# Two-layer transformer on one core: expert gathers, row combinations, splines and norms of the second layer's attention, placed in smaller pieces over more steps

## The chip, the cores and the metric

The kernel runs on one core of a Trainium2 chip. The core has five engines with a queue each: TensorE (PE, with PEld for its weight loads), VectorE (DVE), ScalarE (ACT), GpSimd (POOL) and SyncE (SP, which issues most DMAs). An engine executes its queue in order, and instructions of different engines wait for each other through semaphores. The metric is the device time of one execution, in microseconds (us).

## The reference

The reference has two layers over `x` of 4 batches x 512 tokens x 256 features. Each layer modulates its norms with vectors computed from a small input, adds an attention part with a gate, and adds a feed-forward part with a gate.

- Layer 0: a linear attention part, then a mixture of experts. Every token goes to 6 of 32 experts, each expert takes at most 48 tokens, and the weighted rows of its six experts plus a shared expert are added up for each token. In short: `x = x + gb * y`, where `y` is the sum over six rows and the shared part.
- Layer 1: causal attention with 16 heads of 128, softmax and an output product, then a gated FFN. The three weight matrices of this FFN are not given; they are cubic splines through some 2000 control points, and have to be evaluated.

```
h = layernorm(x) * (1 + cb) + sb
x = x + gb * moe(h)                      # layer 0
h = layernorm(x) * (1 + ca) + sa
x = x + ga * attention(h)                # layer 1
h = layernorm(x) * (1 + cb) + sb
x = x + gb * (silu(h @ gate.T) * (h @ up.T)) @ down.T
```

All is computed in 32-bit floats. Tokens lie on partitions: a batch is 4 blocks (`NTT`) of 128 tokens, `xs[b]` is 128 x 4 x 256.

## The kernel before

Layer 0 runs first, up to about 250 us. Its last step is kept for later in parts: the weighted expert rows lie in `ytab` in HBM, and `code` holds which row belongs to which token and rank. For batch 0 the rows are added up in layer 0 already. For batches 1 to 3 that is done during the attention of layer 1, since a batch needs its `x` only when its own heads begin.

The attention of layer 1 is one loop over 64 heads, 16 for each batch, `for n in range(NHD + 1)` (L1504 and on). A pass of it is called a step here. A step of about 11.6 us computes the scores of head `n`, the projections of head `n + 1` (`project`, in four parts), the transposes and the weighted sum of head `n - 1`, a part of the values of the next four heads, and a part of the output product, `LAG` = 7 steps behind. Products of 256-wide blocks are done with seven block products in place of eight. The sums and differences of weight blocks that this needs are called forms; GpSimd makes them with `weight_forms` (L1161 to L1177): `w3` and `w2` of the next head after part 1 of a projection, `w1` and `w4` after part 3. TensorE reads `w3` and `w2` early in the next step (as `P1p` in the profile), and `w1`, `w4` later in it (as `P2p`). The forms have one buffer each, so the next ones wait until TensorE has read the last. `out_prepare` makes the forms for the output product (`oW`, `oF`, `oH`).

The order of TensorE is the order in the program (`manual_schedule`). On the other engines a planner orders the instructions by readiness and its own estimates; `tc.issue_after(x)` keeps an instruction from being placed ahead of `x` on its engine, without a wait. `evicted[n]` is the VectorE instruction that ends the projection of head `n`; it is executed at the end of step `n - 1`. `last_form[0]` is the last form `w1` that was made.

Besides the heads, a step carries pieces of other work:

- `gather(b, r, after)`, L278: the four row blocks of one rank `r` of batch `b`, by four indirect DMAs from GpSimd, each adding 128 rows of 1 KB into `ysum[b][:, i, :]`. Each waits for `evicted[n]`. Batch 1 has them at steps 1 to 6, batch 2 at 12, 13 and 18 to 21, batch 3 at 28, 29 and 34 to 37; so there are four gathers in a step, and the next gather into the same block comes with the next rank.
- `combine(b, after)`, L290: for each of the four blocks `ysum *= gate` and `x += ysum` on VectorE, at steps 10, 26 and 42.
- `norm(b)`, at steps 11, 27 and 43: the layer norm of the next batch (`ln_stats` takes means and variances of four blocks on VectorE, L192 and L193; the power -1/2 is taken on GpSimd, L196; then `xn`), its transposes, and `norm_forms`.
- `spline(u)`, L1118: one 128 x 256 tile of an FFN weight, on every second step from 6 to 52: a multiplication, three multiply-adds, two of half width, and transposes on TensorE at the end of the step. After units 1, 4 and 7 `ffn_forms` makes four forms on GpSimd.
- `ffn_norm(0)` at step 59 in the program. As nothing holds it, the planner places its statistics as soon as `x` of batch 0 is done, in steps 43 and 44.

The FFN of layer 1 follows, from about 1000 us to the end.

## Time and profile before

| what | value |
|---|---|
| median of three runs | 1174.84 us (1174.59 to 1176.95) |
| the profiled execution | 1174.33 us, of which the span 1172.6 us |
| TensorE busy, whole span | 1121.6 us, 96% |
| TensorE busy, 330 to 470 us | 139.27 of 140 us |
| TensorE busy, 470 to 520 us | 48.78 of 50 us |
| TensorE busy, 780 to 1000 us | 219.51 of 220 us |
| VectorE busy, 330 to 470 us | 116.48 of 140 us |
| GpSimd busy, 254 to 330 us | 60.02 of 76 us |
| granted TensorE clock | 0.988 over the span, 1.00 from 300 us on |

The span is the time from the first to the last instruction of the program in the profile. "Busy" is the time in which an engine executes; waiting and issuing are not in it. In lists of waits, "A <- B" means that A stood idle until B was done; when an instruction waits for several others, the last one by the profile is named. A matmul of 128 x 256 appears as two records, started 0.216 us apart; its shown length (0.38 us) overlaps the next one, so starts are what to compare. [...]

### The profile page before, as it was taken

To read this page: it belongs to the slowest core of one execution; us is meant where nothing else is said; L and a number is where in the kernel's file an instruction comes from. 1 tells how busy PE (TensorE), PEld (TensorE's weight loads), DVE (VectorE), ACT (ScalarE), POOL (GpSimd) and SP (SyncE) were. 2 spreads that over 40 slices of the span, in tenths; PEclk is the share of its full clock that TensorE was granted. 3 is DMA by queue.
4 is the path that set the end of the run, shared out by engine and by line. 5 is a ranking of instruction groups with operands and counts; after the bars stand their busy time and mean duration, and the time that the engine had idled before them with its cause. 6 is when DMAs were issued, how large, how long until landed. Compare 5 with 4: busy or idle time off the path is not lost.

```text
span 1172.6 us, 16886 instructions
## 1 busy us (share of the span) xinstructions
PE 1121.6 (96%) x5220; PEld 823.0 (70%) x5220; DVE 860.2 (73%) x2596; ACT 536.3 (46%) x1373; POOL 621.2 (53%) x945
## 2 busy tenths in 40 slices
PE   6888999879999999999999999999999999999998
PEld 2434354457777777777778777777777777888887
DVE  5688623467888788788887888888877677467765
ACT  3542223335555545554555555554555455333321
POOL 3354124328974856965565975444535655344331
PEclk9999899889999999999999999999999999999999
DMA  7801289734421312321221431011010000000001
GB/s 268 285 26 43 83 250 284 227 113 84 88 64 41 76 43 66 75 68 36 66 57 46 94 64 59 26 39 60 28 37 28 19 18 1 1 1 19 18 1 37
DMA packets 80486, 86.10 MB, mean 73 GB/s; under 512 B 12158, under 2 KB 64748, under 8 KB 80268
## 3 DMA queue, kind: packets, MB, share of 16 engines
q1 hardware_dynamic: 65564, 68.10, 18.6%
q0 software_dynamic: 11712, 13.25, 6.8%
q10 hardware_dynamic: 3120, 3.68, 1.0%
q8 instruction: 42, 0.69, 0.2%
q14 instruction: 48, 0.39, 0.1%
HBM read 73.84 MB, written 11.55 MB: 73 GB/s over the span
## 4 chain that ended last, share of the span: by engine, by line
PE 61%; DVE 9%; POOL 3%; ACT 3%; issue 1%; DMA 1%; SPq 0%; ACTq 0%; DVEq 0%; POOLq 0%
PE s L1293 10%; PE o L1334 9%; PE po L1029 7%; PE P0p L1029 6%; PE fP L1029 6%; PE pt L1325 5%; PE P1p L1029 4%; PE P2p L1029 3%; PE acc L1029 3%; PE P0v L1029 3%; PE P2v L1029 2%; PE P1v L1029 2%; POOL ysum L281 1%; DVE spw L1124 1%; DVE nm L1305 1%
## 5 line engine op out<-in xcount | busy, mean ns | idle before, releaser
L1308 ACT ACTIVATE p<-s,nm 128x512 f32<-128x512 f32 (+3 forms) x256 | 135.4, 529 | 117.1 <-DVE nm L1305 115.0
L1293 PE MATMUL s<-qk,qk 128*128 128x512 f32 (+3 forms) x512 | 170.2, 435 | 1.3 <-DVE qk L1201 1.0
L1334 PE MATMUL o<-pT,v 128*128 128x512 f32 (+3 forms) x512 | 148.6, 433 | 0.2 <-DVE u3v L1213 0.2
L1334 PEld LDWEIGHTS o<-pT,v 128*128 128x128 f32 x512 | 96.8, 190 | 55.0 <-issue 30.6
L1327 ACT COPY pT<-pt 128x512 f32<-128x512 f32 (+1 forms) x192 | 98.4, 513 | 68.2 <-PE pt L1325 66.4
L1305 DVE TENSOR_REDUCE nm<-s 128x1 f32<-128x512 f32 (+3 forms) x256 | 124.1, 485 | 4.0
L281 POOL DMA_INDIRECT ysum<-ytab,code x72 | 113.0, 1570 | 20.4 <-issue 15.5
L1310 DVE TENSOR_SCALAR p<-p,den 128x512 f32<-128x512 f32 (+3 forms) x256 | 117.6, 460 | 3.4
L1325 PEld LDWEIGHTS pt<-ident,p 128*128 128x128 f32 x640 | 81.7, 141 | 34.4 <-issue 10.5
L1325 PE MATMUL pt<-ident,p 128*128 128x128 f32 x640 | 101.7, 273 | 0.3 <-DVE p L1310 0.3
L1303 DVE TENSOR_TENSOR s<-s,mask 128x128 f32<-128x128 f32 x256 | 73.5, 287 | 31.2 <-PE s L1293 31.2
L1168 POOL TENSOR_TENSOR w_p<-w_q,w_k 128x128 f32<-128x128 f32 x63 | 38.7, 615 | 87.2 <-ACT t1p L1207 53.0
L1293 PEld LDWEIGHTS s<-qk,qk 128*128 128x128 f32 x512 | 77.5, 191 | 5.9 <-issue 1.5
L1029 PE MATMUL P0p<-hT_a,w_q 128*128 128x256 f32 x252 | 75.0, 379 | 0.0
L1176 POOL TENSOR_TENSOR w_p<-w_k 128x128 f32<-128x128 f32 x63 | 29.9, 475 | 81.0 <-PE P2p L1029 81.0
L1029 PEld LDWEIGHTS P0p<-hT_a,w_q 128*128 128x128 f32 x252 | 47.5, 190 | 33.1 <-issue 29.9
L1309 DVE RECIPROCAL den<-den 128x1 f32<-128x1 f32 x256 | 40.4, 158 | 38.4 <-ACT p L1308 33.6
L1029 PE MATMUL P1p<-fT,w_p 128*128 128x256 f32 x252 | 64.9, 380 | 2.4 <-POOL w_p L1170 1.2
L1345 ACT ACTIVATE oH<-o,bia 128x512 f32<-128x512 f32 x64 | 44.0, 687 | 42.1 <-PE o L1334 41.1
L1201 DVE SCALAR_TENSOR_TENSOR qk<-P0p,bia,u3p 128x256 f32<-128x256 f32 x63 | 30.4, 482 | 37.1 <-ACT qk L1222 36.1
L1037 POOL TENSOR_TENSOR fI<-it 128x256 f32<-128x256 f32 x30 | 21.8, 728 | 67.0 <-DVE it L1623 67.0
L1029 PEld LDWEIGHTS P1p<-fT,w_p 128*128 128x128 f32 x252 | 47.6, 190 | 9.9 <-issue 1.9
(338 smaller groups left out, 2683.2 us busy)
## 6 DMA issues: line engine op xcount, KB each, us to landing
wg<-in_w_gate_up SPq DMA_DIRECT2D x16, 704.0 KB
w_q<-in_w_q SPq DMA_DIRECT2D x64, 128.0 KB
w_k<-in_w_k SPq DMA_DIRECT2D x64, 128.0 KB
w_v<-in_w_v SPq DMA_DIRECT2D x16, 512.0 KB
wd<-in_w_down SPq DMA_DIRECT2D x16, 352.0 KB
basis<-in_basis SPq DMA_DIRECT2D x8, 640.0 KB
planes<-zero SPq DMA_DIRECT2D x4, 768.0 KB
yr<-planes SPq DMA_DIRECT2D x4, 768.0 KB
```

The lines of the kernel that those rows point to most:

```text
L281: ga = nc.gpsimd.indirect_dma_start(out=ysum[b][:, i, :], out_offset=None, in_=ytab[:, :], in_offset=bass.IndirectOffsetOnAxis(ap=code[:, ...
L1029: nc.tensor.matmul(out, lhsT=lhsT, rhs=rhs, start=start, stop=stop, skip_group_check=shared)
L1293: nc.tensor.matmul(s[:, at[i] : c], lhsT=qk[n, 0][:, i * P : (i + 1) * P], rhs=qk[n, 1][:, : (i + 1) * P], start=True, stop=True,)
L1303: nc.vector.tensor_tensor(s[:, e - P : e], s[:, e - P : e], mask, ALU.add)
L1305: nc.vector.tensor_reduce(nm, s[:, e - w : e], AX.X, ALU.max, negate=True)
L1308: nc.scalar.activation(p, s[:, e - w : e], AF.Exp, bias=nm, accum_out=den)
L1309: nc.vector.reciprocal(den, den)
L1310: nc.vector.tensor_scalar_mul(p, p, den)
L1325: nc.tensor.transpose(pt[:, c : c + P], probs[n, i][:, j * P : (j + 1) * P], ident)
L1327: nc.scalar.copy(pT, pt[:, :w])
L1334: nc.tensor.matmul(o[:, j * P :], lhsT=vs[n // 4][:, j, hc : hc + HD], rhs=pTs[n, j], start=(j == 0), stop=(j == NTT - 1),)
L1345: nc.scalar.activation(oT, o, AF.Identity, bias=bia[:, 2, h : h + 1])
```

## The change

Nothing is computed otherwise; where instructions stand is changed.

- `gather` handles one block and one rank, and no longer waits for `evicted[n]`. For each batch the 24 gathers are in the order block by block, the six ranks of a block after each other. At each step at most one is placed after part 2 of the projection, and up to three more after `out_prepare`. Batch 1 has 3, 3, 3, 3, 3, 3, 2, 2, 2 of them from step 0 on; batches 2 and 3 have 3, 3, 1, 1, 1, 1, 3, 3, 3, 3, 1, 1 from steps 12 and 28 on.
- `last_form[0]` is set after the early forms too, so what is placed after it may come behind `w2` as well.
- `combine` handles one block: at steps 3, 5, 7 and 10 for batch 1, at 15, 20, 22 and 25 for batch 2, at 31, 36, 38 and 41 for batch 3. It takes the block's statistics as well, and `ln_stats` uses them.
- `spline(u, part)`: the first three of its six operations are placed on the odd step before, the others and the transposes where the whole was.
- `ffn_forms` for the first three chunks: at steps 10, 26 and 42, after `last_form[0]`.
- `ffn_norm(0)` may not be placed ahead of `evicted[59]`.

```diff
     def ln_stats(b, name, after):
-        st = small.tile([P, NTT, 6], F32, tag="st", name=f"st_{name}{b}")
-        ag = small.tile([P, NTT, 2], F32, tag="ag", name=f"ag_{name}{b}")
-        with after_or_not(after):
-            for i in range(NTT):
-                nc.vector.bn_stats(st[:, i, :], xs[b][:, i, :])
-                nc.vector.bn_aggr(ag[:, i, :], st[:, i, :])
+        if b in stats:
+            _, ag = stats.pop(b)
+        else:
+            ...
-    def gather(b, r, after):
-
-        for i in range(NTT):
-            ga = nc.gpsimd.indirect_dma_start(
-                ...
-            )
-            wait_for(ga, [after])
-
-    def combine(b, after):
-
-        for i in range(NTT):
-            y, xi = ysum[b][:, i, :], xs[b][:, i, :]
-            with tc.issue_after(after.ins):
-                nc.vector.tensor_tensor(y, y, gbr[:, b, :], ALU.mult)
-                nc.vector.tensor_tensor(xi, xi, y, ALU.add)
+    def gather(b, i, r):
+
+        nc.gpsimd.indirect_dma_start(
+            out=ysum[b][:, i, :],
+            out_offset=None,
+            in_=ytab[:, :],
+            in_offset=bass.IndirectOffsetOnAxis(ap=code[:, b * NTT + i, r : r + 1], axis=0),
+            compute_op=ALU.add,
+        )
+
+    def combine(b, i, after):
+        ...
+        with tc.issue_after(after.ins):
+            nc.vector.tensor_tensor(y, y, gbr[:, b, :], ALU.mult)
+            nc.vector.tensor_tensor(xi, xi, y, ALU.add)
+            nc.vector.bn_stats(st[:, i, :], xi)
+            nc.vector.bn_aggr(ag[:, i, :], st[:, i, :])
@@
-        def spline(u):
+        def spline(u, part):
             r, j = divmod(u, 3)
             t, c = basis[r], win[:, j, r, :]
+            if part == 0:
+                w = spw[u] = sp.tile([P, D], F32, tag="spw", name=f"spw{u}")
+                nc.vector.tensor_scalar_mul(w, t[:, 1, :], c[:, 1:2])
+                for q in (2, 3):
+                    nc.vector.scalar_tensor_tensor(w, t[:, q, :], c[:, q : q + 1], w, ALU.mult, ALU.add)
+                return
+            w = spw.pop(u)
+            nc.vector.scalar_tensor_tensor(w, t[:, 4, :], c[:, 4:5], w, ALU.mult, ALU.add)
             ...
@@
-                nc.gpsimd.tensor_tensor(w2, A22, w3, ALU.subtract)
+                new_form = nc.gpsimd.tensor_tensor(w2, A22, w3, ALU.subtract)
                 wc[key] = {2: w2, 3: w3}
+                last_form[0] = new_form
@@
-        gathers = {r + 1: (1, r) for r in range(TOPK)}
-        for b in range(2, B):
-            for r, n in enumerate((-4, -3, 2, 3, 4, 5)):
-                gathers[(b - 1) * NH + n] = (b, r)
+        gathers, combined_at = {}, {}
+        for b in range(1, B):
+            todo, first_step = [(b, i, r) for i in range(NTT) for r in range(TOPK)], (0, 12, 28)[b - 1]
+            for n, m in enumerate((3, 3, 3, 3, 3, 3, 2, 2, 2) if b == 1 else (3, 3, 1, 1, 1, 1, 3, 3, 3, 3, 1, 1)):
+                gathers[first_step + n] = [todo.pop(0) for _ in range(m)]
+            for i, n in enumerate((3, 5, 7, 10) if b == 1 else (3, 8, 10, 13)):
+                combined_at[first_step + n] = b, i
+
+        def gather_some(n, m):
+            with tc.issue_after(last_form[0].ins):
+                for _ in range(min(m, len(gathers.get(n, ())))):
+                    gather(*gathers[n].pop(0))
@@
             project(n + 1, 2)
+            gather_some(n, 1)
@@
                 out_prepare(n)
+            gather_some(n, 3)
@@
+            if n % 2 and 5 <= n and unit < 3 * NCH:
+                with tc.issue_after(evicted[n].ins):
+                    spline(unit, 0)
+            if n in (10, 26, 42):
+                with tc.issue_after(last_form[0].ins):
+                    ffn_forms(n // 16, early[:, n // 16])
             if n % 2 == 0 and 6 <= n and unit < 3 * NCH:
                 with tc.issue_after(evicted[n].ins):
-                    spline(unit)
-                if unit in (1, 4, 7):
-                    ffn_forms(unit // 3, early[:, unit // 3])
+                    spline(unit, 1)
@@
-            if n in gathers:
-                gather(*gathers[n], evicted[n])
+            if n in combined_at:
+                combine(*combined_at[n], evicted[n])
             if n // NH + 1 < B:
-                if n % NH == 10:
-                    combine(n // NH + 1, evicted[n])
@@
-                ffn_norm(0)
+                ffn_norm(0, evicted[n])
```

## The prediction

> **What bounds the kernel now.** I read the page first, then TensorE's list of waits in the attention of layer 2, then busy time by stage, then the timeline at three places.
>
> The page (engine busy times, and the row of the gathers; columns of that row: line, engine, operation, out<-in, count | busy us, mean ns | idle before):
>
> ```profile
> span 1172.6 us, 16886 instructions
> ...
> PE 1121.6 (96%) x5220; PEld 823.0 (70%) x5220; DVE 860.2 (73%) x2596; ACT 536.3 (46%) x1373; POOL 621.2 (53%) x945
> ...
> L281 POOL DMA_INDIRECT ysum<-ytab,code x72 | 113.0, 1570 | 20.4 <-issue 15.5
> ```
>
> TensorE's waits from 300 to 1000 us (who <- for whom: us, times, longest):
>
> ```profile
> PE P2v L1029 <- DVE v L1200: 1.9, 1, 1.9
> PE P2p L1029 <- POOL oWTrue L1361: 1.2, 2, 0.7
> PE P1p L1029 <- POOL w_p L1170: 1.2, 1, 1.2
> PE P1p L1029 <- DVE x L248: 1.1, 2, 0.6
> PE s L1293 <- DVE qk L1201: 0.4, 2, 0.2
> PE pt L1325 <- DVE p L1310: 0.3, 1, 0.3
> ```
>
> TensorE is the bound: in 700 us it stands 6.1 us. So the change, which alters no matmul and no place in TensorE's or SyncE's order (the built programs agree there instruction by instruction), can win little. But every late VectorE or GpSimd result is paid in full.
>
> **The change part by part.** The profiled execution took 1174.33 us, of which 1172.6 are span. The three timed runs have the median 1174.84, 0.5 more. I sum on the span.
>
> *What is taken away.* The 1.2 us of `w_p L1170` come at 506.5: four steps in a row hold four gathers each (7.5 us of GpSimd at the pitch of 1.86 below), and four FFN forms (L1050 to L1053, about 2.4 us there) follow them, ahead of the forms that `P1p` needs. Afterwards the forms are at steps 10, 26 and 42, where no gathers stand: 1.2 won. The 1.9 us at 775.8 is a pile on VectorE: the FFN norm of batch 0, the norm of batch 3 and a spline, with a stand for GpSimd's power in it:
>
> ```profile
> 775.08 0.16 DVE L203 SCALAR_TENSOR_TENSOR nmr_f<-ag_f,rs_f 128x4 f32<-128x4 f32 x1 [0.91 <-POOL rs_f L196]
> ```
>
> The FFN norm moves to step 59, where no spline stands. I count 1.9 won and 0.4 lost again there. The two waits put down to `oWTrue` (385.7, 575.7) sit behind the same pile for batches 1 and 2 (GpSimd had ended; the VectorE read of that PSUM bank was late): statistics now come earlier but the trip to GpSimd for the power stays, so half, 0.6. The waits of `s` on `qk` come just after a spline of six operations in a row; halved splines win 0.3. `x L248` is the residual, untouched. Sum of waits 3.6; around the wait at 506 the matmul starts lose 1.39 for 1.22 of wait, so times 1.14: **4.1 us won** (bounds: 0, and 5.4 if all 4.7 go). VectorE's operations (multiply, add, statistics, splines) keep their number and size; only places move, so no busy time is added.
>
> *What is added: a chain of landings.* Before, a step issues the four row blocks of one rank. The next gather into the same block comes a step later. Now six gathers into one block follow each other, each adds into the same bytes, and in the built program each waits on the semaphore of the one before. What a gather takes until it has landed, the trace shows at the last gather of batch 3: GpSimd's timeline, then DMA share in 40 slices of 0.2 us from 692 to 700:
>
> ```profile
> 689.06 1.56 POOL L281 DMA_INDIRECT ysum<-ytab,code  x1 [0.30 <-issue]
> ...
> 692.79 1.56 POOL L281 DMA_INDIRECT ysum<-ytab,code  x1 [0.30 <-issue]
> 693.77 1.06 POOL L1168 TENSOR_TENSOR w_p<-w_q,w_k 128x128 f32<-128x128 f32 x1
> ...
> DMA  6676545665434333565544420000000000000000
> ```
>
> GpSimd is done after 1.6 us, but packets run to about 697.0, 4.2 us after the start, and the completion signals come after them. In the trace's records of these signals 44 of the 72 gathers have all sixteen: the last comes 4.29 to 6.06 us after the start, mean 4.85; for batch 1's own (266 to 327 us) the median is 4.6. I take landing 4.6 and a link from start to start of 4.75 (0.15 is the idle time that precedes a gather after other GpSimd work). The Trainium skill speaks against me here: "DMA: Bandwidth & Descriptors", section "Anatomy of one DMA — SWDGE (gpsimd) path", fits 2.0 us + bytes/436e3, for 128 KB an estimated 2.3 us. Counted from the start, a link would be shorter than the work between two gathers, the chain would cost nothing and the sum were -4.1. Counted from the end of the 1.56 us it would be 3.86, and the sum -1.5 by the working below. The row was measured on these gathers, so it decides. The same section says that a semaphore wait is spent on the issuing sequencer: GpSimd's queue stands meanwhile. No run here has shown that yet.
>
> *Batch 1 in time.* Steps 0 to 5 carry three gathers each, and the step lasts about 10.5 us (287.32, 308.02, 328.52 are the starts of `s` in steps 3, 5, 7), while three links need 14.2. The first gather can start at 258.2 (after the two forms that now precede it), the second at 265.6 (behind `w_v` L1170, which ends at 265.45). From there, in the new order: four links to the 6th; to the 7th, into a new block, no wait: 1.6 for the gather, 1.0 for the two forms, 0.15 idle = 2.8; five links to the 12th, 2.8, five to the 18th.
> 6th: 265.6 + 4 x 4.75 = 284.6, landed 289.2. 12th: 284.6 + 2.8 + 23.75 = 311.15, landed 315.75. 18th: 311.15 + 2.8 + 23.75 = 337.7, landed 342.3.
> The work between (at most three or four forms, 2.5 us, in a gap of 4.75 - 1.6) fits in. Behind a waiting gather stand the forms of the next head (`P1p` and `P2p` wait for these) and those of the output product (`po` does).
>
> Who waits: the multiply of each row combination, placed on VectorE's queue at steps 3, 5 and 7 for these three blocks, right behind the 384-column `p`. Behind it stands the 256-column `p`, which the first transposes of the step need:
>
> ```profile
> 286.16 0.62 DVE L1310 TENSOR_SCALAR p<-p,den 128x384 f32<-128x384 f32 x1
> ...
> 307.15 0.90 DVE L1310 TENSOR_SCALAR p<-p,den 128x384 f32<-128x384 f32 x1
> ...
> 327.14 0.41 DVE L1310 TENSOR_SCALAR p<-p,den 128x384 f32<-128x384 f32 x1
> ```
>
> ```profile
> 289.48 0.60 PE L1325 MATMUL pt<-ident,p 128*128 128x128 f32 x4
> ...
> 310.18 0.60 PE L1325 MATMUL pt<-ident,p 128*128 128x128 f32 x4
> ...
> 330.68 0.60 PE L1325 MATMUL pt<-ident,p 128*128 128x128 f32 x4
> ```
>
> After the landing come multiply 0.41, reciprocal 0.15, one spline operation 0.5 (at step 3 an add of 0.42) and `p` 0.35: 1.4 us. So the transposes can start at 290.6, 317.15 and 343.7 at the earliest, against 289.48, 310.18 and 330.68: TensorE is **1.1, 7.0 and 13.0 us** late, cumulative. The fourth block (steps 6 to 8, two gathers each, read at step 10) lands in time: about 340 + 5 x 4.9 + 4.6 = 369 against 364.4 + 13. GpSimd's own lateness sits under the same delay: the forms behind the 18th gather end at 340.4 and `P1p` of step 7 wants them at 329.8. It would cost 10.6 alone. So there are two witnesses for one delay. VectorE comes out of each stand with statistics and masks queued: 0.7 more.
>
> In general the delay is 15 x landing - 56 us: 8.5 at 4.3 (the least seen), 19 at 5.0. A slower wake than 0.15 (0.3, twice as much) would add 2.1.
>
> *Batches 2 and 3* have the six gathers of a block with one a step in between, and combine later: first block 395.5 + 5 x 4.75 + 4.6 = 423.9, `p` then at 424.6, transposes at 425.5: covered by 0.9. That cover is gone at landing 4.75, and 5.7 to 6.1 was seen at 580 to 584, beside large loads: I put 0.5 (0 to 3). Their other blocks have over 3 us.
>
> *The rest at nothing:* the halved spline's second part still ends before the transposes at the step's end (the work hiding it is TensorE's 2.2 us of `o`; uncovered it costs about 0.4); FFN forms at 26 and 42 are used in the FFN only, after 1000 us.
>
> Sum: 13.0 + 0.7 + 0.5 - 4.1 = +10.1. Span 1182.7, the profiled execution about 1184.4, a median of **1185 us**.
>
> **The rivals.** (a) *The chain is hidden and only the wins stay*: 1174.8 - 4.1 = 1170.7. For it: stage by stage GpSimd has room (53%), and the page's 2.3 us. Against it: the packets above. It decides below a landing of 4.0 us, where 15 x 4.0 - 56 = 4 equals the wins (below 3.8 for a gain of over 0.2%); none of 44 is under 4.29. (b) *Wins and losses cancel*: 1174.8 within 2.35 us, a landing of 3.8 to 4.1 or wins at 5.4 with part of the stand hidden by VectorE's slack. (c) *The chain is slower still*: 5.0 to 5.2 by the loads of weights at the same time (5.75 at 293), +17 to +20, 1192 to 1195. (d) *It is half of it*, since GpSimd or VectorE have slack that I don't see, with landings near 4.3: +3 to +5, 1178 to 1180.
>
> **How the numbers follow.** Forecast (landing 4.35 to 4.9) 0.66, (a) 0.09, (b) 0.05, (c) 0.08, (d) 0.12. 0.2% or 2.35 us is about what a measurement of this kernel can tell from no change. Faster is (a), 0.09; same (b), 0.05; slower the rest, 0.86. The likeliest case alone spans 1180 to 1190. For 8 in 10 I leave out (a), most of (b) and the far part of (c): 1176 to 1192.
>
> **What would show it.** Right: GpSimd gathers of batch 1 start 4.6 to 4.9 us apart, with idle time ahead of each put down to a gather's landing; the multiply of `ysum` at steps 5 and 7 has 5 to 7 us of VectorE idle before it; TensorE's `pt` or `P1p` wait there, 13 us by step 8, and steps 18 to 22 run without the wait for `w_p`. Wrong: gathers closer than 4 us, or no wait of TensorE before 345 us. Then the span would fall. If the waits at 385, 575 and 775 stay as long, my 4.1 is wrong.

## The result

The kernel after takes 1193.07 us (median of four runs, 1192.12 to 1197.39), the kernel before 1175.88 us beside it: ratio 1.0168, 95% interval 1.0150 to 1.0186. This ratio is not the quotient of the two medians (1.0146); on 1175.88 it is a loss of 19.8 us. The forecast was 1185 with the range 1176 to 1192. The sign was right, and the loss is 17 us by the medians where I had 10.

The page of after, engine busy times and the row of the gathers:

```profile
span 1195.7 us, 16879 instructions
...
PE 1130.4 (95%) x5220; PEld 822.2 (69%) x5220; DVE 892.1 (75%) x2596; ACT 534.1 (45%) x1373; POOL 626.4 (52%) x945
...
L283 POOL DMA_INDIRECT ysum<-ytab,code x72 | 114.4, 1589 | 79.5 <-DMA ysum<-ytab,code 53.2
```

Two things differ from the page of before. GpSimd now sits 79.5 us idle ahead of its gathers (20.4 before), 53.2 of them until an earlier gather has landed. And VectorE is busy for 892.1 us in place of 860.2, with the same 2596 instructions.

TensorE's waits from 300 to 1000 us, as for before (who <- for whom: us, times, longest):

```profile
PE pt L1338 <- DVE p L1323: 7.2, 5, 2.7
PE pt L1338 <- ACT pT L1340: 2.8, 4, 0.9
PE o L1347 <- DVE u3v L1226: 1.9, 3, 1.0
PE pt L1338 <- ACT p L1321: 1.9, 2, 1.0
PE o L1347 <- ACT pT L1340: 1.7, 2, 0.9
PE P2p L1035 <- DVE qk L1214: 1.1, 4, 0.3
```

The transposes `pt` wait for `p` most. The waits of before (`P2v`, `oWTrue`, `w_p` in batch 2, `x`) are gone from the head of the list.

To see where the time went I took from both traces the start of the first 512-column `s` in every step, and compared how long each step lasts. This begins at step 0; the 2.15 us by which the profiled execution of after reaches step 0 later come from work that the change doesn't touch (in the profiled executions below, step 0 starts anywhere from 249.7 to 257.0 us). From step 0 to step 63 the kernel after loses 20.9 us:

| steps | lost or won, us |
|---|---|
| 3 to 9 | 2.65, 2.16, 4.58, 1.09, 3.18, 1.43, 1.15: lost 16.2 |
| 15, 19, 21, 25, 31, 35, 37, 39, 41 | 1.98, 1.28, 0.25, 1.52, 1.75, 1.19, 1.09, 0.88, 1.53: lost 11.5 |
| 59 | lost 0.6 |
| 11, 22, 24, 27, 34, 38, 40, 44 | 0.98, 1.41, 0.34, 0.90, 0.36, 0.43, 0.68, 2.13: won 7.2 |

Small ones that the table leaves out make up the rest. The profiled execution of after is 4.3 us above the median of its four, and that of before 1.5 us below the median of its own; 2.15 of these 5.8 us lie ahead of step 0. So the steps say 21 where the medians say 17.

One trace of a kernel has an uncertainty of its own. Four measurements further down run the kernel before unchanged and append something behind it. Between step 0 and step 63 the order of instructions on TensorE, VectorE, ScalarE and GpSimd is the same in all five, and yet these four take 0.1, 0.5, 2.7 and 3.2 us longer than the execution that serves as reference here: in three of them `s` waits for `qk` at step 34 (1.6 us), and in two step 44 takes 1.7 us more (see the end). A difference of up to 3 us between the sums of two traces is therefore no evidence by itself; a loss at the same step in several kernels is.

In batch 1 the chain of landings looks as forecast. GpSimd's timeline around the twelfth gather (start, us, engine, line, operation, out<-in, [idle before <- for whom]):

```profile
304.21 1.56 POOL L283 DMA_INDIRECT ysum<-ytab,code  x1 [2.34 <-DMA ysum<-ytab,code]
...
308.87 1.56 POOL L283 DMA_INDIRECT ysum<-ytab,code  x1 [0.53 <-DMA ysum<-ytab,code]
309.87 1.04 POOL L1374 TENSOR_TENSOR oWTrue<-wo,oWTrue 128x128 f32<-128x128 f32 x1
310.29 1.04 POOL L1187 TENSOR_TENSOR w_p<-w_q,w_p 128x128 f32<-128x128 f32 x1
313.54 1.56 POOL L283 DMA_INDIRECT ysum<-ytab,code  x1 [2.22 <-DMA ysum<-ytab,code]
```

The links are 4.66 and 4.67 us. VectorE, and then TensorE, at step 5:

```profile
317.87 1.42 DVE L299 TENSOR_TENSOR ysum<-ysum,gbr 128x256 f32<-128x256 f32 x1 [1.59 <-DMA ysum<-ytab,code]
...
319.81 0.34 DVE L1323 TENSOR_SCALAR p<-p,den 128x256 f32<-128x256 f32 x1
```

```profile
320.20 0.55 PE L1338 MATMUL pt<-ident,p 128*128 128x128 f32 x3 [2.56 <-DVE p L1323]
```

The multiply stands for the landing, 256-column `p` stands behind the multiply, and TensorE behind `p`. One sign of the forecast did not come: VectorE is idle for 1.6 to 1.8 us ahead of the three multiplies, not for 5 to 7 at the second and third. TensorE was late by then already: at steps 3, 4 and 6 it had also waited for `u3v`, for `w_p` and for ScalarE's `pT`. And the multiply itself takes 1.42 us where I had put 0.41. That is the first sign of what the forecast left out.

### The profile page after: what moved, and what is told of

It is laid out like the page before. It is cut to its first block, busy times and chain, and to the rows that moved or that the text cites. A ratio compares the mean times of both kernels' runs of the same rounds, so it can differ in the third digit from the quotient of the medians.

```text
span 1195.7 us, 16879 instructions
## 1 busy us (share of the span) xinstructions
PE 1130.4 (95%) x5220; PEld 822.2 (69%) x5220; DVE 892.1 (75%) x2596; ACT 534.1 (45%) x1373; POOL 626.4 (52%) x945
## 4 chain that ended last, share of the span: by engine, by line
PE 44%; DVE 6%; ACT 2%; issue 1%; POOL 0%; ACTq 0%; DVEq 0%
PE o L1347 6%; PE s L1306 6%; PE fP L1035 6%; PE po L1035 5%; PE P0p L1035 4%; PE pt L1338 4%; PE acc L1035 3%; PE P2p L1035 3%; PE P1p L1035 2%; PE P0v L1035 2%; PE P2v L1035 1%; PE P1v L1035 1%; DVE p L1323 1%; DVE spw L1133 1%; DVE nm L1318 1%
## 5 line engine op out<-in xcount | busy, mean ns | idle before, releaser
L283 POOL DMA_INDIRECT ysum<-ytab,code x72 | 114.4, 1589 | 79.5 <-DMA ysum<-ytab,code 53.2
L1323 DVE TENSOR_SCALAR p<-p,den 128x512 f32<-128x512 f32 (+3 forms) x256 | 133.3, 521 | 2.6
L1338 PEld LDWEIGHTS pt<-ident,p 128*128 128x128 f32 x640 | 80.7, 141 | 51.8 <-DVE p L1323 10.6
L1316 DVE TENSOR_TENSOR s<-s,mask 128x128 f32<-128x128 f32 x256 | 73.2, 286 | 15.3 <-PE s L1306 15.1
L1180 POOL TENSOR_TENSOR w_p<-w_q,w_k 128x128 f32<-128x128 f32 x63 | 41.4, 657 | 68.5 <-ACT t1p L1220 36.8
L1189 POOL TENSOR_TENSOR w_p<-w_k 128x128 f32<-128x128 f32 x63 | 39.2, 622 | 61.4 <-PE P2p L1035 61.4
```

The costliest lines, as they stand in the source:

```text
L283: nc.gpsimd.indirect_dma_start(out=ysum[b][:, i, :], out_offset=None, in_=ytab[:, :], in_offset=bass.IndirectOffsetOnAxis(ap=code[:, b * N ...
L1180: nc.gpsimd.tensor_tensor(w3, A11, A21, ALU.subtract)
L1316: nc.vector.tensor_tensor(s[:, e - P : e], s[:, e - P : e], mask, ALU.add)
L1323: nc.vector.tensor_scalar_mul(p, p, den)
L1338: nc.tensor.transpose(pt[:, c : c + P], probs[n, i][:, j * P : (j + 1) * P], ident)
```

## The experiments

Times are medians; a ratio is to runs of the kernel before on the same chip. "Lost" is the loss from step 0 to step 63 against the kernel before, from the profiled executions.

### First: which part of the change loses

**Whole splines in the kernel after.**

```diff
-            if n % 2 and 5 <= n and unit < 3 * NCH:
-                with tc.issue_after(evicted[n].ins):
-                    spline(unit, 0)
...
+                    spline(unit, 0)
                     spline(unit, 1)
```

> The kernel after, with each spline in one piece on the even steps again. Theory of the shared path: in the kernel after, VectorE operations that read only SBUF take up to twice as long beside GpSimd's forms (a spline operation 1.00 us beside forms, 0.48 without), and the first halves of the splines on odd steps meet these forms. Then VectorE's busy time falls from 892 to 875 us or less, the losses of steps 15, 19, 25, 31, 35, 41 (together some 9 us) go down by more than half, and the time is 1184 to 1189. As the prediction had it (halved splines win 0.3 us, no busy time is added): 1193.4. Rival, late landings in batches 2 and 3: steps 15 and 31 lose 2 us each as before, and the time stays at 1192 to 1194.

1191.55 us, ratio 1.0144 (1.0110 to 1.0178), lost 19.6; VectorE busy 877.3 us. The losses of steps 19 and 35 are gone, but steps 15, 25, 31 and 41 still lose 1.2, 1.5, 1.2 and 1.5. So the halved splines explain 15 of VectorE's 32 us, but only 1.3 us in the steps, and in the time nothing that is clear of noise. The theory in this form fell.

**Halved splines alone, in the kernel before** (`spline(u, part)` and its two calls as in the change, nothing else).

> The kernel before, with nothing but the halved splines. Theory of the shared path: VectorE's busy time rises from 860 by 5 us or more and the time by 2 to 6 us, to 1178 to 1182. As the prediction had it: 0.3 us won, 1175.5. If the halves only collide with forms that GpSimd runs in trains after standing for gathers, the kernel before has no such trains, and the time stays within 1 us of 1175.9.

1170.38 us, ratio 0.9951 (0.9938 to 0.9963), won 5.1, although VectorE's busy time rises from 860.2 to 872.5. All three expectations missed it. The gain comes in small steps, 1.56 of it at step 44 and 0.67 at each of 24 and 40. TensorE's waits for `x` (1.1 us before) are no longer in the list, and of that for `v` on VectorE (2.3 from step 0 on, 1.9 of it at step 44) 0.4 is left. Alone, this part beats both kernels.

**Gathers of batch 1 by twos, and its combinations later.**

```diff
+            if b == 1:
+                todo = [(b, 2 * h + i, r) for h in range(2) for r in range(TOPK) for i in range(2)]
...
-            for i, n in enumerate((3, 5, 7, 10) if b == 1 else (3, 8, 10, 13)):
+            for i, n in enumerate((5, 7, 9, 10) if b == 1 else (3, 8, 10, 13)):
```

> The kernel after, where the gathers of batch 1 alternate between two row blocks (the same number in each step), and the combinations of batch 1 stand at steps 5, 7, 9 and 10. Theory of the chain: successive gathers are no longer 4.7 us apart, steps 3 to 9 lose under 4 us in place of 16.2, and the time is 1179 to 1183. Rival, VectorE's work beside GpSimd's forms makes the loss of batch 1 as well: steps 3 to 9 keep 8 us or more of the loss, 1186 to 1191.

1183.05 us, ratio 1.0065 (1.0044 to 1.0086), lost 7.6. Steps 3 to 8 lose 0.9 us in all where the kernel after loses 15.1, and step 9 loses 3.8 (a wait of 1.9, and matmuls at a lower clock behind it, see the end). With the next run, which moves the combinations alone, this shows that the chain of landings makes the loss of batch 1.

**The chain kept, only the combinations later** (second hunk above without the first).

> The kernel after with the order of its gathers (six into one block, each waiting for the one before), but with the combinations of batch 1 at steps 5, 7, 9 and 10, so that VectorE has no landing to wait for. Two witnesses, as the prediction had it: GpSimd's own lateness still costs 10.6 us by step 8, TensorE waits for the forms (P1p and P2p on w_p) in place of pt, and the time is 1189 to 1192. If VectorE's stand carries the loss alone: like the kernel with two blocks, 1179 to 1183.

1195.50 us, ratio 1.0174 (1.0141 to 1.0207), lost 23.6. VectorE has no landing to wait for, and nothing is won. GpSimd's waits from 255 to 345 us, and TensorE's from 300 to 1000:

```profile
POOL ysum L283 <- DMA ysum<-ytab,code: 28.3, 14, 2.9
```

```profile
PE pt L1338 <- ACT pT L1340: 5.1, 5, 2.5
PE o L1347 <- DVE u3v L1226: 4.6, 4, 2.1
PE pt L1338 <- DVE p L1323: 4.3, 4, 1.8
```

GpSimd stands for landings all the same (20.0 us in the kernel after). Its late forms reach TensorE by way of `u3v`, and a 256-column `p` takes 2.38 us at step 5 (0.35 alone): GpSimd is the "second witness" of the prediction, and by itself it costs as much as both together. (Some 3 of the 23.6 us belong to two stretches at half clock, see the end.) Waits of TensorE for `w_p`, which I expected, are not in the list. Take VectorE's stand away, and GpSimd's remains.

### Second: the wins, and the row combinations

**FFN forms moved and FFN norm held, alone.**

```diff
-                if unit in (1, 4, 7):
-                    ffn_forms(unit // 3, early[:, unit // 3])
+            if n in (10, 26, 42):
+                with tc.issue_after(last_form[0].ins):
+                    ffn_forms(n // 16, early[:, n // 16])
...
-                ffn_norm(0)
+                ffn_norm(0, evicted[n])
```

> The kernel before, with the FFN forms at steps 10, 26 and 42 and the FFN norm of batch 0 held to step 59, and nothing else of the change. As the prediction had these two parts: the wait of 1.2 us at step 21 and the pile of 1.9 us at step 44 go, 0.4 is lost at step 59, times 1.14: 3 us won, ratio 0.9975. The kernel after won 1.4 and 2.1 us at these two steps and lost 0.6 at step 59. Rival: these wins belong to the halved splines and the spread statistics, since the kernel with halved splines alone had won 1.6 us at step 44 already: under 1.5 us in all.

1174.57 us, ratio 1.0003 (0.9987 to 1.0020), won 1.1 in the trace: 0.90 at step 22 and 2.13 at step 44 won, 0.56 at step 59 lost as forecast, and 0.9 at step 43 and 0.6 at steps 28 and 29 lost anew. Not measurable in time: the rival (under 1.5 us) comes nearest.

**The same with halved splines.**

> The kernel before, with halved splines, the FFN forms at steps 10, 26, 42 and the FFN norm held: no change to gathers and combinations. Halved splines alone won 5.1 us between step 0 and step 63. If the wins add up: 5.1 + 1.4 + 0.5, about 7 us, ratio 0.994. If they are the same win twice: as halved splines alone, ratio 0.995 to 0.996.

1169.87 us, ratio 0.9951 (0.9934 to 0.9968), won 5.4. The step times show both wins at steps 22 and 44 (1.49 and 2.13), with losses elsewhere; against halved splines alone nothing measurable is added: the same win twice. The two kernels are the best that I ran.

**Row blocks combined at steps 8 and 10 with their statistics**, added to that kernel.

```diff
-                if n % NH == 10:
-                    combine(n // NH + 1, evicted[n])
+                if n % NH in (8, 10):
+                    for i in range(n % NH - 8, n % NH - 6):
+                        combine(n // NH + 1, i, evicted[n])
```

> As the kernel with halved splines, FFN forms and FFN norm moved, and in addition two row blocks combined at step 8 and two at step 10 of each batch, with their statistics beside them (no landing to wait for, even steps). If early statistics take the waits at the norms (1.3 us put down to oWTrue) away without new waits: 1 to 1.5 us better than without. If a combination costs VectorE's queue wherever it stands: 1 to 4 us worse than without.

1173.68 us, ratio 0.9988 (0.9975 to 1.0001), won 1.0: 3.8 us above the kernel without. Step 10 of each batch loses 1.3 to 1.6, the steps of the norms (11 and 27) win 0.98 and 0.90.

**All four at step 8.**

> As the kernel with halved splines, FFN forms and FFN norm moved, with all four row blocks and their statistics combined at step 8 of each batch. With two blocks at step 8 and two at step 10, step 8 lost 0.1 and step 10 1.3 to 1.6 us, and the norms won 0.98 and 0.90. If only step 10 is a bad place (the norm behind it): 1.5 us better than without early combinations, ratio 0.9938. If the queue pays for every combination with statistics: 1 to 3 us worse, 0.996 to 0.998.

1170.68 us, ratio 0.9965 (0.9954 to 0.9975), won 4.2. The norms' wins stay (0.98, 0.90 and, at step 43, 0.93), and the combinations cost about 1.3 us a batch at steps 8 and 9. So early statistics win 0.9 to 1.0 at each norm and cost somewhat more: 1.2 us in all by the traces, while the times (1170.68 and 1169.87) don't differ beyond noise.

### Third: where batches 2 and 3 lose

**Combinations of batches 2 and 3 on even steps** (`(4, 8, 10, 14)` for `(3, 8, 10, 13)`), on the kernel with two alternating blocks.

> The kernel with two alternating row blocks in batch 1, and the combinations of batches 2 and 3 on even steps (16, 20, 22, 26 and 32, 36, 38, 42 in place of 15, 20, 22, 25 and 31, 36, 38, 41). Theory: the losses at steps 15, 25, 31 and 41 (1.74, 1.52, 1.74 and 1.52 us) come from a combination, the first half of a spline and GpSimd's train of forms for the output product meeting on odd steps; on even steps they go, and the time is 1176 to 1179 (from 1183). Rival 1, a combination costs TensorE as much wherever it stands: 1182 to 1184. Rival 2, at steps 15 and 31 the landing of the sixth gather is late: only these two losses go, 1179.5.

1181.05 us, ratio 1.0049 (1.0021 to 1.0077), lost 3.6, between the theory and its first rival. The losses of steps 25 and 41 are gone, those of 15 and 31 fall from 1.74 to 1.13 and 0.99, although no combination is left there. What steps 25 and 41 lost in the kernel after was late VectorE work, beside the combination and the first half of a spline. TensorE at step 25:

```profile
569.87 0.67 PE L1035 MATMUL P2p<-fT,w_p 128*128 128x256 f32 x2 [0.31 <-DVE qk L1214]
...
573.19 0.67 PE L1035 MATMUL P2p<-hT_a,w_p 128*128 128x256 f32 x2 [0.26 <-DVE qk L1214]
```

Neither landing nor parity is the whole cause.

**All combinations at 10, 26 and 42: the gathers' new places alone.**

```diff
-                combined_at[first_step + n] = b, i
+                combined_at.setdefault(NH * b - 6, []).append((b, i))
```

> The kernel with two alternating row blocks in batch 1, with all combinations at steps 10, 26 and 42 as in the kernel before (with their statistics). Left over are the new places and order of the gathers in batches 2 and 3. Theory, gathers that stand between GpSimd's forms delay and bunch them, and the bunches hold VectorE: steps 15, 31, 21, 37 and 39 still lose about 1 us each, and the time is 3 us or more above the kernel with all four blocks combined at step 8, that is 1175 to 1179. If the combinations at odd steps alone make these losses: within 1 us of it, 1170 to 1172.

1177.15 us, ratio 1.0009 (0.9990 to 1.0029), lost 1.7: 5.9 more than the kernel with the gathers in their old places and the combinations at step 8. Steps 15, 19, 21, 31, 35 and 37 lose 1.52, 1.13, 0.84, 1.13, 1.36 and 0.59. These are 6.6 of the 11.5 us that batches 2 and 3 lose: more than half comes from the places and the order of the gathers.

What the gathers do to VectorE can be seen in the kernel after at step 15. VectorE, then GpSimd beside it:

```profile
440.35 2.08 DVE L1131 TENSOR_SCALAR spw<-basis,win 128x256 f32<-128x256 f32 x1
...
442.43 0.86 DVE L299 TENSOR_TENSOR ysum<-ysum,gbr 128x256 f32<-128x256 f32 x1
443.22 0.81 DVE L1323 TENSOR_SCALAR p<-p,den 128x256 f32<-128x256 f32 x1
```

```profile
439.31 1.56 POOL L283 DMA_INDIRECT ysum<-ytab,code  x1
440.31 1.05 POOL L1189 TENSOR_TENSOR w_p<-w_k 128x128 f32<-128x128 f32 x1
440.73 1.04 POOL L1377 TENSOR_TENSOR oWFalse<-wo 128x128 f32<-128x128 f32 x1
441.15 1.03 POOL L1378 TENSOR_TENSOR oWFalse<-wo,oWTrue 128x128 f32<-128x128 f32 x1
441.56 1.44 POOL L1387 TENSOR_TENSOR oF<-oH 128x256 f32<-128x256 f32 x1
```

A spline operation of 0.34 us takes 2.08, and `p` behind it is late. VectorE waits for no data here: its row shows no idle time. TensorE waits for that `p`:

```profile
444.08 0.55 PE L1338 MATMUL pt<-ident,p 128*128 128x128 f32 x3 [0.67 <-DVE p L1323]
```

Over the whole attention, 256-column `p` takes 0.35 us without forms beside it and 0.78 beside forms (31 of 64); in the kernel before it was 0.36 and 0.56 (40 of 64). Operations that read PSUM (`qk` 0.48, `u2p` 0.42) take the same in both kernels. Summed over all of VectorE's operations from step 0 to step 63, those beside forms take 31 us longer in the kernel before than the median of the same operation without forms, and 66 us longer in the kernel after. That covers the growth of 32 us.

**VectorE beside GpSimd, by itself** (behind the kernel's last product: four operations of each kind with GpSimd idle, then the same beside sixteen GpSimd subtractions; this measurement and the three of this kind below ran once each).

> The kernel before, with a measurement behind its last product (not part of the result): four scalar_tensor_tensor and four tensor_scalar of 128x256 f32 that read only SBUF and four scalar_tensor_tensor that read PSUM and SBUF, on VectorE, first with GpSimd idle, then beside sixteen GpSimd subtractions of 128x256 without a gap. Theory of the shared path: with GpSimd idle 0.48, 0.35 and 0.48 us; beside GpSimd the SBUF-only ones are held to the end of what GpSimd has begun or longer (together 5 us or more in place of 3.3), the PSUM ones stay at 0.48. If the long durations in the kernel after come from waits for data: the same durations in both rounds.

VectorE's timeline, first with GpSimd idle, below beside it (the time is for four):

```profile
1167.03 2.04 DVE L1760 SCALAR_TENSOR_TENSOR probe_v<-probe_v,probe_c,probe_v 128x256 f32<-128x256 f32 x4
1169.11 1.52 DVE L1762 TENSOR_SCALAR probe_v<-probe_v,probe_c 128x256 f32<-128x256 f32 x4
...
1173.40 3.41 DVE L1760 SCALAR_TENSOR_TENSOR probe_v<-probe_v,probe_c,probe_v 128x256 f32<-128x256 f32 x4
1176.85 3.10 DVE L1762 TENSOR_SCALAR probe_v<-probe_v,probe_c 128x256 f32<-128x256 f32 x4
1179.98 2.04 DVE L1764 SCALAR_TENSOR_TENSOR probe_v<-probe_p,probe_c,probe_v 128x256 f32<-128x256 f32 x4
```

6.51 us in place of 3.56 where only SBUF is read, and 2.04 unchanged where PSUM is read. The Trainium skill has the rule behind this, in "SBUF — State Buffer", section "SBUF: two separate sides": VectorE, in a 2-port mode or with two SBUF inputs, and GpSimd share a pair of SBUF ports, and whoever starts first has it for a whole instruction. The row agrees: sixteen subtractions take 13.0 us, 0.81 each, and each VectorE operation that reads only SBUF took 0.70 to 0.83. But 2.08 us is more than one instruction's worth.

**Gathers in the second program.**

> The kernel before, with a second measurement behind its last product (not part of the result): VectorE scalar_tensor_tensor of 128x256 f32 that read only SBUF (0.50 us with GpSimd idle), beside four GpSimd programs in turn: three gathers into different tiles; gather and three 128x128 forms, three times, into different tiles; the same into one tile, so that each gather waits for the landing of the one before; twelve forms alone. In the kernel after, VectorE operations of this kind were lengthened by 0.2 us on average and 1.6 at most beside forms, by 0.47 and up to 3.0 where a gather and forms follow each other. Theory, gather and forms in one train hold VectorE longest: single operations of 1.2 to 3 us in the second program, at most 0.8 in the first and the last. In the third: short while GpSimd stands for the landing, long in the trains behind it. If each form alone holds VectorE for its own length: 0.5 to 0.8 us in the last program, no operation above 1 us in any.

The planned order did not come about: the gathers don't depend on what the forms read, and six of them were issued in a row ahead of the forms. Beside gathers alone VectorE's operations took 0.48 us, beside forms that overwrite one tile 0.56, twice 0.78. No long operation; not decisive for the second program.

**The same with the order fixed.**

> The kernel before, with a third measurement behind its last product (not part of the result): VectorE scalar_tensor_tensor of 128x256 f32 that read only SBUF (0.48 us with GpSimd idle), beside four GpSimd programs in turn: sixteen 128x128 forms of which each overwrites the one before; sixteen forms of which five in a row write different tiles; a gather and five forms into different tiles, three times; a gather and five forms that overwrite each other, three times. Theory, an unbroken train holds VectorE to its end: forms that overwrite each other leave a gap of 0.08 us into which VectorE gets, 0.56 us each, in the first and the last program; behind a gather the next forms have been issued while it runs (1.05 us in the trace, begun 0.41 apart), no gap is left, and single VectorE operations of 1.2 to 2.5 us stand in the third program; in the second 0.6 to 1. If the long operations in the kernel after are not made by GpSimd's trains: no operation over 0.8 us in any program.

In all four programs VectorE's operations took 0.48 to 0.58 us (the first of a program 0.78): no long one, also behind gathers. While VectorE asks without a break, VectorE and GpSimd take turns, and GpSimd's forms come 0.59 us apart in place of 0.41. The expectation missed.

**Single operations, as the attention has them** (each SBUF-only operation between two that read PSUM).

> The kernel before, with a fourth measurement behind its last product (not part of the result): on VectorE a scalar_tensor_tensor that reads PSUM (0.48 us) and one operation that reads only SBUF take turns, 128x256 f32, as in the attention, beside GpSimd forms of 128x128: sixteen in a row with scalar_tensor_tensor and with tensor_scalar, then three times a gather and five forms with the same two. Where VectorE's SBUF-only operations followed each other without a break, VectorE and GpSimd took turns (0.56 us each). Theory: an SBUF-only operation that comes while a train of forms is on waits until the train leaves a gap: single operations of 1.2 to 2.5 us here, as in the kernel after. If VectorE gets in after each form here too: at most 0.9 us, and what makes the long ones in the kernel after stays open.

VectorE and GpSimd in the third program:

```profile
1196.51 0.65 DVE L1769 SCALAR_TENSOR_TENSOR probe_v<-probe_v,probe_c,probe_v 128x256 f32<-128x256 f32 x1
1197.09 0.47 DVE L1765 SCALAR_TENSOR_TENSOR probe_v<-probe_p,probe_c,probe_v 128x256 f32<-128x256 f32 x1
1197.48 2.24 DVE L1769 SCALAR_TENSOR_TENSOR probe_v<-probe_v,probe_c,probe_v 128x256 f32<-128x256 f32 x1
1199.65 0.47 DVE L1765 SCALAR_TENSOR_TENSOR probe_v<-probe_p,probe_c,probe_v 128x256 f32<-128x256 f32 x1
```

```profile
1195.89 1.82 POOL L1783 DMA_INDIRECT probe_y<-ytab,code  x1 [0.17 <-issue]
1197.14 2.87 POOL L1790 TENSOR_TENSOR probe_w<-probe_ga,probe_v 128x128 f32<-128x128 f32 x5
```

An operation that comes while five forms behind a gather are on ends 0.3 us before the last of them: 2.24, 2.17 and 2.14 us in the third program, 1.98 three times with `tensor_scalar` in the fourth. Without a gather ahead of the forms (first and second program) the same operations take 0.34 to 0.69. So a train of forms directly behind a gather holds a single VectorE operation nearly to its end.

In the kernel before, no `p` and no spline operation takes more than 0.96 us, although gathers stand ahead of forms there too. 54 of its 72 gathers have another gather directly behind them, and 15 of the other 18 the forms `w3` and `w2`, of which the second reads the first and begins only when that has ended:

```profile
326.88 1.56 POOL L281 DMA_INDIRECT ysum<-ytab,code  x1 [0.30 <-issue]
327.88 1.06 POOL L1168 TENSOR_TENSOR w_p<-w_q,w_k 128x128 f32<-128x128 f32 x1
329.01 0.45 POOL L1170 TENSOR_TENSOR w_p<-w_k,w_p 128x128 f32<-128x128 f32 x1
```

The change puts most gathers ahead of forms that don't depend on each other. That fits the holds; it was not tested by itself, except for the run with gaps below.

**Gathers only at the end of a step.**

```diff
-            gather_some(n, 1)
```

> The kernel with the gathers in their new steps and all combinations at steps 10, 26 and 42, but each step issues all its gathers at its end, behind the forms of the output product, and none in the middle of the step. Theory, a gather directly ahead of a train of forms (in the middle of the step) makes the train late and unbroken: the losses at steps 15, 19, 21, 31, 35 and 37 (1.5, 1.1, 0.8, 1.1, 1.4 and 0.6 us) fall to a third or less, and the time goes from 1177.2 to 1172 to 1174. Rival, GpSimd's load is what counts, wherever the gathers stand in the step: 1176 to 1178.

1176.77 us, ratio 1.0015 (0.9998 to 1.0031), lost 3.0: as with a gather in the middle, and as the rival had it. But one VectorE operation is lengthened by 2.35 us here too, since the gathers now stand ahead of other forms. So this run doesn't separate the theories.

**A gap behind each gather of batches 2 and 3.**

```diff
+        if b > 1:
+            t = small.tile([P, 2], F32, tag="gap", name=f"gap{b}{i}{r}")
+            with tc.issue_after(ga.ins):
+                nc.gpsimd.tensor_tensor(t, nhalf[:, 0:2], nhalf[:, 2:4], ALU.subtract)
+                nc.gpsimd.tensor_tensor(t, t, nhalf[:, 0:2], ALU.subtract)
```

> The kernel with the gathers in their new steps and all combinations at steps 10, 26 and 42, and behind each gather of batches 2 and 3 two 128x2 operations on GpSimd, the second of which waits for the first, so that the forms behind them are no longer issued while the gather runs. Theory, a train of forms behind a gather holds a VectorE operation to its end: the time VectorE loses beside gathers with forms (10.5 us) falls, the losses at steps 15, 19, 21, 31, 35 and 37 (6.6 us in all) fall to under half, and the time goes from 1177.2 to 1173 to 1175. Rival, GpSimd's load and lateness cost the time: two more operations per gather make it 1177 to 1180.

1176.47 us, ratio 0.9999 (0.9984 to 1.0015), lost 1.3. The planner left one form between gather and gap in 14 of 48 cases. The time is no better beyond noise, and the steps tell why. The losses of steps 15, 19, 31 and 35 (5.1 us together) are gone to the last hundredth, and VectorE's busy time falls from 883.3 to 869.7. Step 21 now loses 2.5 and step 37 4.9. There `o` waits for `u3v` for 2.25 and 3.21 us; `u3v` reads the product `P1v`, which needs late forms, and GpSimd still waits 37.6 us for landings from 400 to 800 us. So the holds make the losses of steps 15, 19, 31 and 35 in this kernel; at steps 21 and 37, with three gathers a step, GpSimd's own lateness takes over. The spline operation of step 15 without the gap, then with it:

```profile
422.36 2.07 DVE L1131 TENSOR_SCALAR spw<-basis,win 128x256 f32<-128x256 f32 x1
```

```profile
422.29 0.38 DVE L1136 TENSOR_SCALAR spw<-basis,win 128x256 f32<-128x256 f32 x1
```

**The ranks of all four blocks in turn, in batches 2 and 3**, with the same number of gathers in each step.

```diff
+            else:
+                todo = [(b, i, r) for r in range(TOPK) for i in range(NTT)]
```

> The same kernel without these two operations, with the gathers of batches 2 and 3 in the order of the kernel before (four row blocks of one rank, then the next rank; the same number in each step as in the kernel after). If the chain of landings makes the losses of batches 2 and 3 too (gathers that stand, and trains behind them): the 6.6 us fall to 3 or less, 1172 to 1174.5. If what counts is that gathers stand in these steps at all: 1176 to 1178.

1172.23 us, ratio 0.9968 (0.9939 to 0.9997), won 2.7: 4.4 better in the steps than with the blocks' order. Only steps 19 and 35 still lose 1.1 and 1.0, each with a spline operation of 2.04 us. From 400 to 800 us GpSimd waits for no landing, where it waited 39.6 us with the blocks' order. So the order block by block costs time in batches 2 and 3 too.

From the best kernel to the kernel after, the parts cost in the steps (us): early statistics and combinations 1.2 (from 5.4 to 4.2 won), new steps for the gathers 1.5, the order block by block in batches 2 and 3 4.4, spread combinations 1.9, those on odd steps 4.0 (1.7 of it a lower clock in one step), block by block with early combinations in batch 1 13.3. Each is the difference of two single traces: 13.3 is far beyond what traces of one kernel differ by, 4.4 is borne out by the times (1177.15 and 1172.23), and the others are not shown one by one. New steps and early combinations overlap, too: the run with ranks in turn combines at step 10, the one before it at 8.

## Why the prediction was right and wrong

**The chain of landings in batch 1: right.** Links of 4.75 were 4.6 to 5.0. The 18th gather started at 339.5 where I had 337.7, or 339.9 with the later step 0. The landing was 4.46 us in the median. The transposes of steps 3, 5 and 7 came 1.2, 7.8 and 13.7 us late; I had 1.1, 7.0 and 13.0. Part of this lateness came by other waits than the multiply's, but the landing sets its sum. Taking the chain away takes away 14.2 of 15.1 us in steps 3 to 8. The rule of the skill that I had weighed (2.3 us by "DMA: Bandwidth & Descriptors", section "Anatomy of one DMA — SWDGE (gpsimd) path") would have been a wrong guide to the time; its other sentence, that a wait is spent on the issuing queue, the trace of after shows with 53.2 us.

**"Two witnesses for one delay": half right.** GpSimd's side alone costs as much as both together (lost 23.6 against 20.9, times 1195.50 and 1193.07), not 10.6 of 13. Beside the late forms, which I had counted, operations of VectorE are held there too (`p` for 2.38 us).

**"0.7 more" behind the stands: too small.** Steps 3 to 9 lost 16.2 where I had 13.7. The multiply that I put at 0.41 us took 0.59, 1.42 and 1.48, and at step 8 a 128-column `p` took 3.26.

**"Batches 2 and 3: 0.5 (0 to 3)": this term failed, and it made the sum wrong.** They lost 11.5. I asked when a block has landed, and found the time sufficient. I did not ask what gathers between forms do to GpSimd's queue where nobody waits for the block. The gathers' places and order make 6.6 of it at six steps: at four of these (5.1 us) trains of forms behind gathers hold VectorE, which the gap shows; at the other two late forms hold TensorE. Behind it stands the chain of landings again, on GpSimd's queue: with the ranks in turn most of these losses go. The spread combinations bring the rest; at steps 25 and 41 (3.0) they make `qk` late. The split is measured in kernels that combine later than the kernel after; within the kernel after itself it was not.

**"No busy time is added", "only places move": this failed too, and lies under that term.** VectorE's busy time grew by 32 us at the same number of instructions, since SBUF-only operations are held by GpSimd's forms. The trace of before had shown it: 256-column `p` at 0.56 us beside forms against 0.36. I took one duration from the rows, and never asked what stood beside. Busy time as such is not the cost, though: the halved splines add 12 us of it to the kernel before and win 5.1. A hold costs when it stands ahead of something that TensorE waits for.

**"4.1 us won": too small.** The steps won 7.0 net of step 59 (7.2 in the table, 0.4 in small ones, less 0.6), beyond the bound of 5.4. `w_p` (1.2, times 1.14) was right with 1.41, the pile with 2.13, step 59 with 0.57. The norms won 1.9, not half of 1.2. The halved splines, which I put at 0.3, are worth 5.1 alone in the kernel before, though not in the kernel after; and with them alone the wait for `x L248`, which I had called untouched, is gone. A small wait in the list isn't a bound on what a shorter queue wins.

Sum: 10.1 in the forecast, less 2.9 for the wins, plus 2.5 in batch 1, plus 11.0 in batches 2 and 3, is 20.7 against 20.9 in the steps. That the error was no larger is in part luck, since the larger wins covered 2.9 of it. Of the rivals, (c), a slower chain, came nearest in time (1192 to 1195), but not for its reason: the landings were no slower than forecast. Its sum was also about 1 us too high: at 5.0 it is 19 + 1.2 - 4.1 = 16.1, not 17.

## What to carry to other kernels

If GpSimd gathers into one tile several times, put the gathers of other tiles in between: a gather that waits for a landing holds everything behind it on that queue, and moving the reader did not help here. Before VectorE or GpSimd work is moved, see what stands beside it: an operation that reads only SBUF has two durations, and the mean of a row hides them. A step whose data is in time can still lose by what its instructions do to the queue and to the neighbour engine; and parts of a change that win alone should be measured alone.

## What I had not expected of the hardware

- A train of GpSimd forms directly behind an indirect gather kept a single VectorE operation that reads only SBUF busy for 1.98 to 2.24 us (0.34 and 0.47 alone), six times out of six; the same train without the gather did not, and a VectorE that asks without a break was let in after each form. Why is open: in the trace the forms behind a gather last 1.05 us and begin 0.41 apart, so that the next has begun before the last ends. Two small operations that depend on each other, placed behind the gather, ended it at steps 15, 19, 31 and 35.
- After a long wait (1.9 to 3.2 us here) TensorE sometimes runs at a lower clock. In the kernel with gaps, behind the wait of 3.21 us (columns of this stage table: stretch, us, busy us of TensorE, its weight load, VectorE, ScalarE and GpSimd with their counts, granted clock, DMA share, GB/s):

```profile
685.00:691.00 6.00, 6.00 (x33) 5.14 (x32) 3.95 (x13) 2.62 (x8) 4.85 (x8) 1.00 0.21 32
691.00:696.00 5.00, 1.79 (x9) 1.24 (x8) 1.20 (x5) 1.51 (x5) 4.26 (x9) 0.91 0.41 88
696.00:700.00 4.00, 4.00 (x10) 2.11 (x10) 2.69 (x9) 1.05 (x3) 2.47 (x5) 0.68 0.13 18
```

  The granted clock falls to 0.68, and the matmuls there lost 1.55 us beside the wait. A wait of 1.93 us had this behind it in one kernel (0.77), and one of the same length in another had not (1.00); nor had waits of 2.56 and 2.67 in the kernel after. The kernel before shows that it isn't the program: its wait of 1.9 us for `v` at step 44 is in all five executions. In two of them a stretch of 3.4 us at half clock follows, and the step takes 1.7 us more; in three the clock stays at 1.00. One of the two, from the execution with the second measurement behind it:

```profile
782.40:785.80 3.40, 3.40 (x8) 2.00 (x7) 2.40 (x9) 1.52 (x5) 1.07 (x2) 0.50 0.00 0
```

  What decides is open; the length of the wait alone does not.
